# Projection evicted one image at a time, rows dealt by h mod 4, 1 KB runs and tables written in stage A, in a two-layer conv block

## The chip, the cores and the metric

The kernel runs on one core of one Trainium2 chip. The metric is the device time of one execution in microseconds. Before the change it is 4737.04 us, the median of three runs (4735.08 to 4738.93). Everything is float32.

A core has TensorE (PE, with its weight loads shown apart as PEld), VectorE (DVE), ScalarE (ACT), GpSimd (POOL) and SyncE (SP). In this kernel SP and POOL do little but issue DMAs. DMAs issued on SP and on POOL go through two queues that share the core's 16 DMA engines.

## The reference

The input `x` is (16, 192, 64, 64): 16 images, 192 channels, 64 rows `h`, 64 columns `w`.

```python
# layer 0
h = layernorm_over_channels(x, eps=1e-6) * ln1_w + ln1_b
projected, gate = split(conv1x1(h, in_proj_w) + in_proj_b)       # 192 -> 384
projected = depthwise3x3(projected, dw_k)                        # zero padded
decay  = clip(sigmoid(decay_logits), 0.05, 0.995)                # 4 x 192
mix    = softmax(mix_logits, axis=0);  iscale = 1 + tanh(input_scale)
# s[i] = decay*s[i-1] + (1-decay)*iscale*projected[i]
scanned = mix[0]*scan_right + mix[1]*scan_left + mix[2]*scan_down + mix[3]*scan_up
mixed = (scanned + depthwise3x3(projected, le_k)) * sigmoid(gate)
mixed = gelu(batchnorm_over_images_and_pixels(mixed, eps=1e-5) * bn_w + bn_b)
x = x + conv1x1(mixed, out_proj_w) + out_proj_b
h2 = layernorm_over_channels(x)
x = x + fc2(gelu(fc1(h2)))                                       # 192 -> 768 -> 192
# layer 1
t = relu(bn(mean_over_pixels(x) @ w1.T));  taps = t @ w2.T + b2  # per image
x = depthwise3x3(x, taps * mask) + bias                          # 4 of 9 taps are not 0
```

The batch norm needs all images before any pixel can go on, so the kernel has one full stop between the part in front of it and the part behind it.

## The kernel before

**Set-up (L107 to L195).** The 192 channels lie as three classes of 64. Biases, decays and gains are worked out from the parameter table; `wi` (the projection's weights, scaled by the layer norm's weights, with the mean taken off) is made; `bias_bc` (L144) holds the projection's bias on all partitions. Depthwise taps, local taps and the two horizontal scans are written as eight vectors of 128 per channel (`gv`, `gt`), from which banded 64x64 matrices can be read by an overlapping access pattern; they are stored to DRAM as `dv_d` (3 stores, L192) and `lv_d` (5 stores, L194) on the SP queue.

**Stage A (L197 to L265).** The work is cut into 64 chunks: two images, one in each half of the partitions, by 8 rows (512 pixels). `load_a` (L208) brings a chunk on SP with two DMAs of 2 KB runs into one of three `xa` buffers, issued two chunks ahead. `stat_a` (L218) transposes it on TensorE and takes the layer norm's statistics on VectorE. `project` (L235) does four groups of 128 pixels: one PSUM tile `ps_pj` of two banks holds both images, the output has pixels on the partitions and 384 channels along a row. Of each image VectorE evicts the projected half with scale and bias (`stt`, L246, which the profile shows at L64), ScalarE the gate half (L247), so both engines read the same bank. Results go to `stg`, two tiles of [128, 384, 16] per block; a block is four chunks (32 rows of two images). When a block is complete, four DMAs on POOL (L252) store it to `pg_d` with 24 KB per partition. A partition holds a column `w` and the parity of the row: row 32 jb + 2 j + parity.

**Stage B (L268 to L398).** 24 groups of 8 channels, 96 iterations of two channels each; now `w` is on the partitions, eight images in each half. `load_b` (L285) loads a group on SP: four DMAs of `pg_d` with 512 byte runs into `p_b` and `g_b`, and the tables `dm` (L299) and `lm` (L302); two buffers of each. One iteration has: `depthwise` (L305), seven parts of banded matmuls (L324 to L328, run by L315) into two `ps_d` tiles, copied to `q` by ScalarE (L331); `scans` (L334), the two vertical scans on VectorE (L343, L345) with a decay table written by ScalarE (L339); `local` and `vertical` (L354, L362, run by L352), which add the local taps, both horizontal scans and both vertical scans in `ps_l`; `gate` (L366), the sigmoid (L373), the product into `o_b` (L377) and the batch norm's statistics (L378). After four iterations two DMAs on POOL (L382) store the group to `mixed_d`.

**Batch norm and stage C (L401 on).** The statistics are put together (L408 to L437), then the pool `early` is closed (L438), and in the space that this frees the weights of the rest are loaded on SP (L440 to L459), with a few products made from them (L470 to L478). Stage C goes over 64 chunks of two images by 8 rows: load of x and of mixed (y), out projection, layer norm, fc1, gelu, fc2, and per image the second layer's taps.

**What sets the order.** TensorE's instructions run in the order in which the code issues them (`manual_schedule(engines=PE_ORDER)`); a tile scheduler orders VectorE and ScalarE by readiness. DMAs of one queue are issued in order, and an issue that has to wait for a free buffer holds back what is behind it on SP or POOL.

Of the kernel before, what the change touches and what calls it, by code (L numbers as in the profile page):

```python
# [21 lines left out]
F32 = mybir.dt.float32  # L22
# [21 lines left out]
AR = CR // 2  # L44

# [7 lines left out]
def conv_block_kernel(ctx: ExitStack, tc: tile.TileContext, x, prm, w_in, w_out, w_fc1, b_fc1, w_fc2, w1, bn1, w2, out):  # L53
# [22 lines left out]
    pg_d = dram.tile([n_img_all, NB, HW, 2 * C * BR], F32, tag="pg_d", name="pg_d")  # L76
# [7 lines left out]
    load_cls3(pt3, prm)  # L84

# [6 lines left out]
    eps5 = cp.tile([128, 1], F32, tag="eps5", name="eps5")  # L92
    nc.vector.memset(eps5, 1e-5)
# [3 lines left out]
    bias_bc = ce.tile([128, 2 * C], F32, tag="bias_bc", name="bias_bc")  # L97
    dec_b = ce.tile([128, 2, C // 2], F32, tag="dec_b", name="dec_b")
    stats = ce.tile([128, C, 6], F32, tag="stats", name="stats")


    with ExitStack() as stage:
        ka = stage.enter_context(tc.tile_pool(name="ka", bufs=1))
        wi = ka.tile([128, 3, 2 * C], F32, tag="wi", name="wi")
        load_cls3(wi, w_in)

        with tc.tile_pool(name="ps_set", bufs=1, space=PSUM) as ps0, tc.tile_pool(name="sset", bufs=1) as sp:  # L107
            lo = slice(0, 64)

# [21 lines left out]
            dg = sp.tile([64, 3, 4, 64], F32, tag="dg", name="dg")  # L131
            lnb = sp.tile([64, 3, 128], F32, tag="lnb", name="lnb")
            for t in range(3):
                for k, v in enumerate((pt3[lo, t, INB:INB + 1], pt3[lo, t, GTB:GTB + 1], dec[:, t, 2:3], dec[:, t, 3:4])):
                    nc.vector.tensor_scalar_mul(dg[:, t, k], ident[lo, lo], v)
                nc.vector.tensor_scalar_mul(lnb[:, t], ones[lo], pt3[lo, t, LN1B:LN1B + 1])
            pb = ps0.tile([128, 2 * C], F32, tag="pb", name="pb")
            for t in range(3):
                nc.tensor.matmul(pb, lnb[:, t], wi[lo, t], start=(t == 0), stop=False)
            for t in range(3):  # L140
                for k in range(2):
                    c0 = k * C + 64 * t
                    nc.tensor.matmul(pb[:, c0:c0 + 64], ones[lo], dg[:, t, k], start=False, stop=(t == 2 and k == 1))
            nc.vector.tensor_copy(bias_bc, pb)  # L144
            pd = ps0.tile([128, 2, C], F32, tag="pd", name="pd")
            for t in range(3):
                for k in range(2):
                    nc.tensor.matmul(pd[:, k, 64 * t:64 * t + 64], ones[lo], dg[:, t, 2 + k],
                                     start=(t == 0 and k == 0), stop=(t == 2 and k == 1))

            for i, q in enumerate(HALF):
                nc.vector.tensor_copy(dec_b[q].rearrange("p k (g c) -> p k g c", c=GC // 2),
                                      pd[q].rearrange("p k (g i c) -> p k g i c", i=2, c=GC // 2)[:, :, :, i])


            for t in range(3):
                nc.vector.tensor_scalar_mul(wi[:, t], wi[:, t], pt3[:, t, LN1W:LN1W + 1])
# [3 lines left out]
            for t in range(3):  # L161
                nc.tensor.matmul(pc, mean_w, wi[lo, t], start=(t == 0), stop=(t == 2))
            for t in range(3):
                nc.vector.tensor_sub(wi[:, t], wi[:, t], pc)
# [20 lines left out]
            gt = sp.tile([128, 8, C], F32, tag="gt", name="gt")  # L185
# [5 lines left out]
            for k in range(3):  # L191
                nc.sync.dma_start(dv_d[:, k].rearrange("g s c -> s g c"), gt[:, k].rearrange("s (g c) -> s g c", c=GC))  # L192
            for k in range(5):
                nc.sync.dma_start(lv_d[:, :, k].rearrange("g i s c -> s (g i) c"),  # L194
                                  gt[:, 3 + k].rearrange("s (g c) -> s g c", c=GC // 2))  # L195
# [8 lines left out]
        xr = x.rearrange("b (t p) h w -> b p t (h w)", p=64)  # L204
# [3 lines left out]
        def load_a(n):  # L208
            p, c = divmod(n, NCH)
            xa = xp.tile([128, 3, CH], F32, tag="xa", name="xa")  # L210
            for i, q in enumerate(HALF):
                nc.sync.dma_start(xa[q], xr[2 * p + i, :, :, c * CH:(c + 1) * CH])
# [22 lines left out]
        def project(n):  # L235
# [3 lines left out]
            for g in range(AR):  # L239
                ps = psa.tile([128, 2, CH], F32, tag="pj", name="ps_pj", bufs=2)  # L240
                for t in range(3):
                    for i, q in enumerate(HALF):
                        nc.tensor.matmul(ps[:, i, 0:2 * C], pixels(n, t, g)[q], wi[q, t], start=(t == 0), stop=(t == 2))  # L243
                for i in range(2):
                    j, r = part * AR + g, ast[n]["rs"][:, g, i:i + 1]
                    stt(stag[blk][i][:, 0:C, j], ps[:, i, 0:C], r, bias_bc[:, 0:C])  # L246
                    nc.scalar.activation(stag[blk][i][:, C:2 * C, j], ps[:, i, C:2 * C], AF.Identity, scale=r)  # L247
            if part == per - 1:
                p, jb = divmod(blk, NB // 2)
                for i in range(2):  # L250
                    for par, q in enumerate(HALF):
                        nc.gpsimd.dma_start(pg_d[2 * p + i, 2 * jb + par], stag[blk][i][q].rearrange("p o j -> p (o j)"))  # L252
                stag.pop(blk)

        with tc.manual_schedule(engines=PE_ORDER):
            for n in range(-1, n_ac):
# [7 lines left out]
                if n >= 0:  # L264
                    project(n)  # L265


    with ExitStack() as stage:  # L268
        kb = stage.enter_context(tc.tile_pool(name="kb", bufs=1))

        mask = kb.tile([128, 2, 2 * CH], F32, tag="mask", name="mask")
        nc.vector.memset(mask, 1.0)
        for k, r in ((0, 0), (1, HW - 1)):
            nc.vector.memset(mask[:, k].rearrange("p (i h) -> p i h", h=HW)[:, :, r:r + 1], 0.0)
# [6 lines left out]
        n_blk = n_half * NB  # L281
# [3 lines left out]
        def load_b(g):  # L285
            s = grp[g]
            s["p"] = gp.tile([128, n_blk, GC, BR], F32, tag="pb", name="p_b")
            s["g"] = gp.tile([128, n_blk, GC, BR], F32, tag="gb", name="g_b")
            for k, dst in ((0, s["p"]), (1, s["g"])):
                lo = (k * C + g * GC) * BR  # L290
                for i, q in enumerate(HALF):
# [431 lines left out]
```

## Time and profile before

| what | value |
|---|---|
| median of the runs | 4737.04 us |
| the profiled execution: its time; its span | 4739.38 us; 4737.6 us |
| set-up, to the first statistics matmul | 0 to 82 us |
| stage A, compute | 82 to 1031 us |
| nothing but DMA | 1031 to 1083 us |
| stage B, 96 iterations | 1083 to 1890 us |
| batch norm, weights, first chunk | 1890 to 1987 us |
| stage C | 1987 to 4738 us |
| busy, share of the span: PE, PEld, DVE, ACT, POOL | 84, 38, 55, 37, 4% |
| mean granted TensorE clock | 0.942 |
| DMA | 500.35 MB, 106 GB/s over the span |

In the profile, a group is named by its line, engine, operation and tiles as output<-inputs, with the mean length of one instruction and what ended the idle time before it. A releaser "DMA xa<-in_x_dram" means that the engine waited for that load. The granted clock is the share of full speed that TensorE was given. The DMA share is the mean busy share of the 16 DMA engines; it can come out slightly above 1.

### The profile page before, as it was taken

Reading aid. Unit: us, or ns where it says so; the run is one execution under the profiler, and the core shown is the slowest. Engines: PE = TensorE matmul, PEld = TensorE weight load, DVE = VectorE, ACT = ScalarE, POOL = GpSimd, SP = SyncE. Lnnn points to the kernel's source line nnn. Section 1 sums busy time; section 2 is a strip of 40 time slices with the busy share of each in tenths; the row PEclk is TensorE's granted clock in tenths of the full one; section 3 lists DMA queues with packets and bytes.
Section 4 is the critical chain, followed back from the end, with each engine's and each line's share of the span. In section 5 each row is a group of like instructions: output and inputs, shape, how many; then the busy total and the mean of one; then the engine's idle time right before and its main releaser. Section 6 shows DMA issues by size and latency. Waiting matters only on the chain.

```text
span 4737.6 us, 59020 instructions
## 1 busy us (share of the span) xinstructions
PE 3959.5 (84%) x24876; PEld 1779.4 (38%) x24876; DVE 2619.0 (55%) x3862; ACT 1753.0 (37%) x2045; POOL 201.6 (4%) x336
## 2 busy tenths in 40 slices
PE   4666766648999998499989999899899899999990
PEld 2444434425555555133333333333333333333330
DVE  3444444436888888344554644744745645546427
ACT  1333333324555555133333433333433333334322
POOL 0000000000000000000000000100100000000001
PEclk9888898888999999699999999999999999999995
DMA  9555666559999996311221221311311212212103
GB/s 46 160 160 160 160 160 160 160 138 230 228 236 237 231 241 152 96 34 47 60 70 37 71 58 38 93 35 47 87 39 48 74 47 58 72 38 66 48 1 98
DMA packets 381896, 500.35 MB, mean 106 GB/s; under 512 B 55056, under 2 KB 268304, under 8 KB 377536
## 3 DMA queue, kind: packets, MB, share of 16 engines
q1 hardware_dynamic: 346496, 289.99, 27.9%
q0 software_dynamic: 35136, 206.59, 15.9%
q8 instruction: 196, 3.21, 0.3%
q14 instruction: 68, 0.56, 0.0%
HBM read 289.17 MB, written 207.36 MB: 105 GB/s over the span
## 4 chain that ended last, share of the span: by engine, by line
PE 45%; DVE 19%; ACT 5%; DMA 5%; issue 3%; SPq 1%; POOL 0%; ACTq 0%; DVEq 0%; POOLq 0%
PE ps_f L584 19%; PE ps_f L506 17%; PE ps_o L506 6%; DVE o L64 5%; DVE v L345 4%; DVE v L343 4%; DMA out_dram<-o 3%; DVE o_b L377 2%; ACT q L331 2%; ACT sg L373 2%; PE ps_m L506 1%; DVE stats L378 1%; ACT o L644 1%; PE ps_v L506 1%; DMA y<-mixed_d 1%
## 5 line engine op out<-in xcount | busy, mean ns | idle before, releaser
L584 PE MATMUL ps_f<-h,wf 64*128 64x512 f32 x4608 | 1054.4, 604 | 17.1 <-DVE h L574 17.1
L506 PE MATMUL ps_f<-gl,wf 128*64 128x512 f32 x4608 | 1021.5, 592 | 0.0
L584 PEld LDWEIGHTS ps_f<-h,wf 64*128 64x128 f32 x4608 | 437.2, 189 | 638.4 <-issue 579.4
L243 PE MATMUL ps_pj<-wi,xa 64*128 64x384 f32 x3072 | 545.9, 502 | 105.1 <-ACT stg L247 105.1
L506 PEld LDWEIGHTS ps_f<-gl,wf 128*64 128x64 f32 x4608 | 330.5, 137 | 658.9 <-issue 658.1
L587 ACT ACTIVATE gl<-ps_f,bf 128x1024 f32<-128x1024 f32 x384 | 425.1, 1109 | 320.7 <-PE ps_f L584 319.9
L545 DVE SCALAR_TENSOR_TENSOR ximg<-ps_o,pt,x 128x512 f32<-128x512 f32 x192 | 144.1, 751 | 610.8 <-PE ps_o L506 610.8
L64 DVE SCALAR_TENSOR_TENSOR o<-ximg,taps,o 128x1024 f32<-128x1024 f32 x318 | 402.2, 1278 | 95.6 <-ACT o L644 91.0
L243 PEld LDWEIGHTS ps_pj<-wi,xa 64*128 64x128 f32 x3072 | 294.2, 192 | 331.4 <-ACT stg L247 154.8
L64 DVE SCALAR_TENSOR_TENSOR stg<-ps_pj,rsa,bias_bc 128x192 f32<-128x192 f32 x512 | 265.2, 535 | 273.0 <-ACT stg L247 166.2
L506 PE MATMUL ps_o<-mx,wo 128*64 128x512 f32 x1536 | 380.9, 617 | 40.8 <-ACT mx L536 14.0
L247 ACT ACTIVATE stg<-ps_pj,rsa 128x192 f32<-128x192 f32 x512 | 287.3, 583 | 301.4 <-DVE stg L64 297.4
L573 DVE RECIPROCAL rs<-rs 128x512 f32<-128x512 f32 x64 | 214.5, 3352 | 297.6 <-ACT rs L572 297.6
L315 PE MATMUL ps_d<-p_b,dm 64*64 64x256 f32 (+3 forms) x5376 | 300.6, 366 | 57.4 <-DMA dm<-dv_d 57.4
L339 ACT ACTIVATE tab<-mask,dec_b 128x1024 f32<-128x1024 f32 x192 | 220.4, 1149 | 319.0 <-DVE v L343 221.8
L315 PEld LDWEIGHTS ps_d<-p_b,dm 64*64 64x64 f32 x5376 | 267.7, 196 | 142.2 <-issue 140.8
L343 DVE TENSOR_TENSOR_SCAN v<-tab,q 128x1024 f32<-128x1024 f32 x96 | 220.1, 2292 | 175.9 <-ACT q L331 175.9
L223 PE MATMUL ps_xt<-ident,xa 128*128 128x128 f32 x768 | 119.4, 316 | 236.6 <-DMA xa<-in_x_dram 233.8
L228 DVE BATCH_NORM_STATS2 st<-ps_xt 128x6 f32<-128x192 f32 x512 | 165.8, 337 | 257.5 <-PE ps_xt L223 197.0
L352 PE MATMUL ps_l<-q,lm 64*64 64x504 f32 (+1 forms) x2304 | 275.9, 604 | 2.8 <-ACT q L331 2.8
L561 ACT ACTIVATE sq<-h 128x1536 f32<-128x1536 f32 x64 | 94.8, 1482 | 466.9 <-DVE h L558 466.9
L352 PE MATMUL ps_l<-v,lm 64*64 64x512 f32 x1536 | 211.9, 617 | 66.3 <-DVE v L345 66.2
(132 smaller groups left out, 2976.7 us busy)
## 6 DMA issues: line engine op xcount, KB each, us to landing
pg_d<-stg POOLq DMA_DIRECT2D x64, 1536.0 KB, 19.8
out_dram<-o POOLq DMA_DIRECT2D x212, 256.0 KB, 3.7
xa<-in_x_dram SPq DMA_DIRECT2D x128, 384.0 KB
p_b<-pg_d SPq DMA_DIRECT2D x48, 1024.0 KB
g_b<-pg_d SPq DMA_DIRECT2D x48, 1024.0 KB
mixed_d<-o_b POOLq DMA_DIRECT2D x48, 1024.0 KB, 12.4
x<-in_x_dram SPq DMA_DIRECT2D x128, 384.0 KB
y<-mixed_d SPq DMA_DIRECT2D x128, 256.0 KB
```

The source lines that it names most:

```text
L64: nc.vector.scalar_tensor_tensor(o, in0, scalar, in1, ALU.mult, ALU.add, **kw)
L243: nc.tensor.matmul(ps[:, i, 0:2 * C], pixels(n, t, g)[q], wi[q, t], start=(t == 0), stop=(t == 2))
L247: nc.scalar.activation(stag[blk][i][:, C:2 * C, j], ps[:, i, C:2 * C], AF.Identity, scale=r)
L315: nc.tensor.matmul(dst(ps[ih][o]), s["dm"][q, di + 1, :, ch], src(s["p"][q, :, ch]), start=(di == 0), stop=stop)
L339: nc.scalar.activation(tab, mask[:, d], AF.Copy, scale=dec_b[:, d, k:k + 1])
L343: nc.vector.tensor_tensor_scan(vf, tab, q, 0.0, ALU.mult, ALU.add)
L345: nc.vector.tensor_tensor_scan(vf[:, ::-1], tab[:, ::-1], q[:, ::-1], 0.0, ALU.mult, ALU.add)
L352: nc.tensor.matmul(dst(bst[k]["ps"][i][o]), grp[g]["lm"][q, m, :, c], src(q, ih), start=start, stop=stop)
L506: nc.tensor.matmul(ps[q], w(i), rhs(i), start=start, stop=stop)
L573: nc.vector.reciprocal(rs, rs)
L584: nc.tensor.matmul(pf[:, i], wf1[q, t, 128 * m:128 * m + 128], s["h"][q, t], start=(t == 0), stop=(t == 2))
L587: nc.scalar.activation(gl, pf, AF.Gelu, bias=bf1[:, m:m + 1])
```

## The change

It touches set-up, stage A, stage B and the place where the weights of stage C are loaded. Line numbers behind "now" are those of the changed kernel.

- **Rows.** Rows are dealt by h mod 4 in place of parity: block `u` of a pair of images holds rows 4 j + 2 u + r, r on the partition halves. A chunk's 512 pixels are now four pairs of neighbouring rows, so its x load has 512 byte runs and is split into six DMAs.
- **Eviction.** Each image has its own PSUM tile and is evicted whole, 384 channels in one instruction: image 0 by VectorE (now L357), image 1 by ScalarE (now L358), with the scale only.
- **Bias.** The projection's bias moves behind the depthwise conv: constant values pass through the conv as the sum of its taps, and differ in the first and last row and column. Set-up works out `bias_q` (inside, correction for the first row, for the last row), and ScalarE's copy of `ps_d` to `q`, one instruction now, adds it, with two small instructions for the edge rows (now L449, L451). `bias_g` keeps the gate's bias.
- **Layout.** The channels' order in `pg_d` is group by group, projected beside gate, so that stage B's runs are 1 KB. `pg_d` is split in two tensors: groups 0 and 1, and the other 22; a block is stored by eight DMAs in place of four. Group 0 is fetched back during stage A into its own buffer, `pg_even`, by `fetch_pair` (now L160) on POOL, one DMA per pair of images.
- **Stage B's buffers and order.** Three buffers hold projected and gate together; the product is written over the projected part, and the store leaves from there, so there is no `o_b`. Loads run two groups ahead. The depthwise conv has five parts in place of seven. It runs two iterations ahead of `vertical` and `gate` where it ran one ahead, and the scans of an iteration come before the next depthwise.
- **Set-up and weights.** The eight stores to `dv_d` and `lv_d` and the weights of stage C are issued inside stage A's loop; products made from the weights (`finish_weights`) too. Space for the weights is no longer shared with stages A and B.

The diff, cut to its core:

```diff
+    def load_weights():            # the loads that stood behind early.close()
+        ...
+    def finish_weights(pb):        # s1, the sums pb, bf1 and wf1: unchanged statements
+        ...
+    pg_even = pf.tile([128, n_blk, 2, GC, BR], F32, tag="pg_e", name="pg_e")
+    def fetch_pair(p):
+        q, i0 = HALF[2 * p // n_half], 2 * p % n_half
+        nc.gpsimd.dma_start(pg_even[q, i0 * NB:(i0 + 2) * NB].rearrange("p n k c j -> p n (k c j)"),
+                            pg_d[0][2 * p:2 * p + 2, :, :, 0:GE].rearrange("i b w e -> w (i b) e"))
...
+            for k in range(3):
+                pr = ps0.tile([3, C], F32, tag="pb", name="pr")
...
+                pq = ps0.tile([128, C], F32, tag="pd", name="pq")
+                nc.tensor.matmul(pq, indt, svt, start=True, stop=True)
+                by_half(bias_q[:, k], pq)
...
-            for k in range(3):
+        def store_vectors(k):
+            if k < 3:
                 nc.sync.dma_start(dv_d[:, k].rearrange("g s c -> s g c"), gt[:, k].rearrange("s (g c) -> s g c", c=GC))
...
-        xr = x.rearrange("b (t p) h w -> b p t (h w)", p=64)
+        xr = x.rearrange("b (t p) (j u r) w -> b u p t j (r w)", p=64, u=2, r=2)
...
             for i, q in enumerate(HALF):
-                nc.sync.dma_start(xa[q], xr[2 * p + i, :, :, c * CH:(c + 1) * CH])
+                for t in range(3):
+                    nc.sync.dma_start(xa[q, t].rearrange("p (g n) -> p g n", n=128),
+                                      xr[2 * p + i, u, :, t, part * AR:(part + 1) * AR])
...
-                for i in range(2):
-                    j, r = part * AR + g, ast[n]["rs"][:, g, i:i + 1]
-                    stt(stag[blk][i][:, 0:C, j], ps[:, i, 0:C], r, bias_bc[:, 0:C])
-                    nc.scalar.activation(stag[blk][i][:, C:2 * C, j], ps[:, i, C:2 * C], AF.Identity, scale=r)
+                j, rs = part * AR + g, ast[n]["rs"]
+                nc.vector.tensor_scalar_mul(stag[blk][0][:, :, j], ps[0], rs[:, g, 0:1])
+                nc.scalar.activation(stag[blk][1][:, :, j], ps[1], AF.Copy, scale=rs[:, g, 1:2])
             if part == per - 1:
...
+                for d, o0, o1 in ((0, 0, GF * 2 * GC), (1, GF * 2 * GC, 2 * C)):
+                    for i in range(2):
+                        for par, q in enumerate(HALF):
+                            nc.gpsimd.dma_start(pg_d[d][2 * p + i, 2 * u + par],
+                                                stag[blk][i][q, o0:o1].rearrange("p o j -> p (o j)"))
+                if u == 1 and p >= 1:
+                    fetch_pair(p - 1)
+                if p == n_pairs - 1 and u == 1:
+                    fetch_pair(p)
...
                     project(n)
+                if n == 3:
+                    load_weights()
+                if 8 <= n < 16:
+                    store_vectors(n - 8)
+                if n == 16:
+                    finish_weights(psa.tile([128, NFC], F32, tag="pb2", name="pb2"))
...
+            s["pg"] = pg_even if g % 3 == 0 else pg_odd[g % 3 - 1]
...
+            blocks = lambda a: a.rearrange("p (i b) j -> p i b j", b=NB)
+            rows4 = lambda a: a.rearrange("p (i j b) -> p i b j", b=NB, j=BR)
+            part(0, blocks, rows4)
+            part(-1, lambda a: blocks(a)[:, :, 0:NB - 1], lambda a: rows4(a)[:, :, 1:NB])
+            part(-1, lambda a: blocks(a)[:, :, NB - 1, 0:BR - 1], lambda a: rows4(a)[:, :, 0, 1:BR])
...
-            for ih in range(2):
-                nc.scalar.copy(q[:, ih], ps[ih])
+            edge = lambda a, r: a.rearrange("p k (i h) -> p k i h", h=HW)[:, :, :, r]
+            nc.scalar.activation(q, ps, AF.Identity, bias=bias_q[:, 0, k:k + 1])
+            for e, r in ((1, 0), (2, HW - 1)):
+                nc.scalar.activation(edge(q, r), edge(ps, r), AF.Identity, bias=bias_q[:, e, k:k + 1])
...
-            load_b(0)
-            for k in range(-1, n_bp + 1):
+            for g in range(3):
+                load_b(g)
+            for k in range(-2, n_bp + 1):
                 if k >= 1:
                     vertical(k - 1)
                     gate(k - 1)
-                if k + 1 < n_bp:
-                    if (k + 1) % hp_ == 0 and (k + 1) // hp_ + 1 < NCG:
-                        load_b((k + 1) // hp_ + 1)
-                    depthwise(k + 1)
+                    if k % hp_ == 0 and k // hp_ + 2 < NCG:
+                        load_b(k // hp_ + 2)
+                if 0 <= k + 1 < n_bp:
                     scans(k + 1)
+                if k + 2 < n_bp:
+                    depthwise(k + 2)
                 if 0 <= k < n_bp:
                     local(k)
```

The scheduler moves issues that wait for nothing: in the changed program as built, SP's first DMAs are the parameters and `w0`, the weights, three `dv_d` and two `lv_d` stores, then the x loads of chunks 0 to 2, then the other three `lv_d` stores.

## The prediction

> **What bounds the kernel now.** I read the mean of each engine by stage first (busy time in given stretches), because one share over the whole span hides three stages with different limits. Columns: stretch and its length, busy us (instructions) of PE, PEld, DVE, ACT, POOL; then granted clock, DMA share, GB/s. Stage A is 82 to 1031 us, B 1083 to 1890, C 1987 to the end.
>
> ```profile
> ...
> 40.00:80.00 40.00, 0.00 (x0) 0.00 (x0) 0.00 (x0) 0.00 (x0) 0.00 (x0) 1.00 1.48 21
> ...
> 300.00:500.00 200.00, 142.21 (x836) 85.86 (x838) 96.03 (x347) 66.12 (x125) 8.49 (x16) 0.90 0.56 150
> ...
> 1031.00:1083.00 52.00, 0.02 (x2) 0.05 (x2) 0.00 (x0) 5.38 (x6) 0.76 (x2) 0.51 1.01 209
> ...
> 1300.00:1500.00 200.00, 182.56 (x2320) 110.64 (x2312) 169.90 (x146) 116.45 (x145) 13.03 (x12) 1.00 1.03 235
> ...
> 2400.00:4600.00 2200.00, 2097.47 (x9672) 756.23 (x9674) 1153.36 (x1254) 783.90 (x705) 77.54 (x146) 0.98 0.19 54
> ```
>
> Stage C is TensorE at 95%; no line of its loop changes. A is 71% TensorE with nothing else full: it waits. B has TensorE at 91% and VectorE at 85%, coupled. 40 to 80 us and 1031 to 1083 us have no compute at all.
>
> Next, order of time on TensorE in A (start, length, line, count, idle before and what ended it):
>
> ```profile
> 375.27 1.53 PE L223 MATMUL ps_xt<-ident,xa 128*128 128x128 f32 x12
> 376.73 4.14 PE L243 MATMUL ps_pj<-wi,xa 64*128 64x384 f32 x24
> 382.73 5.83 PE L243 MATMUL ps_pj<-wi,xa 64*128 64x384 f32 x24 [1.86 <-ACT stg L247]
> 388.49 1.53 PE L223 MATMUL ps_xt<-ident,xa 128*128 128x128 f32 x12
> 389.95 4.14 PE L243 MATMUL ps_pj<-wi,xa 64*128 64x384 f32 x24
> 395.90 4.14 PE L243 MATMUL ps_pj<-wi,xa 64*128 64x384 f32 x24 [1.81 <-ACT stg L247]
> 411.17 2.79 PE L223 MATMUL ps_xt<-ident,xa 128*128 128x128 f32 x12 [11.13 <-DMA xa<-in_x_dram]
> ```
>
> Two waits are seen. In each chunk TensorE waits about 1.8 us for an eviction: the whole list of waits has ScalarE waiting for VectorE's half of the same bank 436 times (297.4 us). And once per block of four chunks the x load is late: 178.6 us in 15 times. The DMA queues say why. In 388 to 394 us only the 24 KB store packets move (1.40 MB). In the next ten us:
>
> ```profile
> q0 software_dynamic: 116, 2.36, 93.0%
> q1 hardware_dynamic: 148, 0.29, 7.6%
> ```
>
> (packets, MB, share): the load gets about one 2 KB packet for each 24 KB store packet, so it lands when the store burst is over, 35.9 us after the block's boundary at 375.27. The load issued at 375.3 is through by 381, since the stores only flow from 379.9.
>
> In B I read one iteration (8.29 us):
>
> ```profile
> 1407.72 2.27 DVE L345 TENSOR_TENSOR_SCAN v<-tab,q 128x1024 f32<-128x1024 f32 x1
> ...
> 1408.28 1.04 PE L352 MATMUL ps_l<-v,lm 64*64 64x512 f32 x8
> ...
> 1410.05 1.15 PE L352 MATMUL ps_l<-v,lm 64*64 64x512 f32 x8 [0.73 <-DVE v L345]
> ...
> 1411.02 3.08 PE L315 MATMUL ps_d<-p_b,dm 64*64 64x512 f32 x56
> ...
> 1413.81 2.29 DVE L343 TENSOR_TENSOR_SCAN v<-tab,q 128x1024 f32<-128x1024 f32 x1 [1.19 <-ACT q L331]
> ...
> 1413.93 2.82 PE L352 MATMUL ps_l<-q,lm 64*64 64x512 f32 x24
> ```
>
> VectorE waits 1.19 us for q, q for the depthwise matmuls, these for the second vertical product, and that (0.73 us) for the scan: a ring through three engines, though none is full.
>
> **The change, part by part**, against this execution: 4739.38 us, of which the span is 4737.6 and 1.8 lies around it; the median shown (4737.04) is 2.3 lower.
>
> *Setup and start of A.* Before, the 8 table stores with 16 and 32 byte packets keep the DMA busy from 20 to 72 us and the first x load lands at 82.4. Moved into A, they are not all gone from the front: in the changed program's SP order the 11 weight loads (beside the 3 of pv, there before), then 3 dv_d and 2 lv_d stores still stand ahead of the first x load. Rate: 44 us for 5 lv_d = 8.8 each, 8 us for 3 dv_d. The set-up arithmetic grows (about 45 small DVE rows at 0.13 us, and three rounds TensorE to VectorE at about 2 us, worked side by side with the rest): from 27.6 to an estimated 36 us. The weights, 2.2 MB at some 235 GB/s = 10 us, fit in the idle DMA time at 8 to 20 us. First x: 38 + 2 x 8.8 + 4 = 60, so -22. The other 3 lv_d (26 us) stand between x chunks 2 and 3; chunk 3 lands at about 99 and is wanted at 85: +14. With a chunk that is 1.3 us shorter four times (below), the first block boundary comes at 121 in place of 135.3: -14. Ends: -30 (set-up no longer) and +5 (all 8 stores ahead of x).
>
> *Eviction.* Per chunk 8 stt (535 ns) and 8 activations (583) of 192 become 4 tensor_scalar and 4 activations of 384, one image each, from their own banks. VectorE, 384 from PSUM into 64 byte steps: between 557 (contiguous copy, L144) and 1082 (twice the strided 192); I take 750, as the strided 192 is nearer to a contiguous 192 (355) than ScalarE's is. ScalarE: 475 (between its contiguous 192 at 319 and 512 at 578) to 1166; I take 1000, since its strided 192 costs 264 more than its contiguous one. Neither engine fills the chunk: VectorE 4 x 0.75 + 2.8 statistics, ScalarE 4.3. TensorE: 1.46 + 4 x 2.03 = 9.6 us; its third group needs the first bank at 5.5, which ScalarE frees at 4.9 + 1.0: 0.5 lost. Chunk 11.5 -> 10.2.
>
> *The x loads and the block.* But the block's length is set by the late load: 35.9 + two chunks = 59.7 on average ((1030.4 - 135.3)/15). Bytes of the burst stay 6.3 MB. SP issues 6 DMAs per chunk in place of 2 (3.7 us in place of 1.2; SP waits most of the time for buffers) and 1536 packets of 512 B; POOL issues 8 stores per block in place of 4 (4.3 us; POOL is idle 95%) and 8 fetches in all, 0.5 MB each, behind the stores: +1 us per block. 512 B packets move at 215 GB/s (stage B, 1412 to 1418 us: 218), 2 KB ones at 229 (82 to 88): no loss worth counting outside the burst. So the first load of the burst (needed after 10.2 us) still slips in ahead of the 22 KB stores (from about 6.1 us), the second lands at 36, and the block is 36 + 2 x 10.2 + 0.5 = 57: 15 x -2.7 = -40. If the first is caught too, the block is 30 + 3 x 10.2 = 60.6: +14. If the burst shortens, 54.5: -78.
>
> The Trainium skill, DMA: Bandwidth & Descriptors, Queues, rings and completion order, says that an engine round-robins between queues by packet. The rows above show nearly that (148 against 116); by it a load with quarter-size packets gets a quarter of the bytes in a burst, which speaks for the caught case and a total of about 4631.
>
> *A to B.* Before 52.6 us: store landing (27.2), 4 MB of group 0, tables. After: landing 27, then the tables (2 x 0.7 MB, first pair about 5 us) beside the last fetch, as group 0's other seven eighths are already in SBUF: 33. Group 1 (4.2 MB at 230 = 18 us, tables 4) comes about 3 us late. -16; ends -26 and 0.
>
> *B.* Parts of the depthwise go from 7 to 5: 16 of 56 matmul instructions with 8 columns go, the 1520 columns stay. By rows, 512 columns take 0.88 us, so 2.6 of the 2.91 is columns: 0 to 0.3 saved, 0.15 taken. The scan moves one iteration away: in the built order VectorE runs scan k+2 next to gate k, so the ring is cut; TensorE's own sum is 2.64 + 1.04 + 0.97 + 2.91 = 7.56, less 0.15 = 7.4; VectorE's is 7.05. ScalarE: q once 1.13 (row 1109 to 1149 for 1024) for 2 x 0.576, plus two of 16 elements at 0.2 to 0.3, 2 x 1.15, 2 x 0.83 = 5.6: covered. DMA per group of four: 4.2 MB pg at 215 to 230, 2.1 MB stores and 1.4 MB tables partly beside each other at 385: 29 to 31 us against 29.6 wanted. It is just covered; if not, 7.75 per iteration. I take 7.45: 96 x -0.84 = -81 (ends 7.2: -105; 7.75: -52). New wait: a load must await the landing (12.4 us) of the store from the same buffer; it is due 44 us after that store's issue, and 12.4 + 19.5 + 4 = 36.
>
> *B to C.* 11 weight DMAs (SP, 1902.2 to 1908.8) and their TensorE sums go; y follows x at once: issued about 9 us earlier, -9 (0 to -15). The moved finish, some 4 us on TensorE at chunk 16, falls into a chunk that has the load's wait behind it: 0, or +4 without that cover.
>
> Sum: -14 - 40 - 16 - 81 - 9 = -160: 4737.6 - 160 + 1.8 - 2.3 = **4577 us**.
>
> The Trainium skill, PSUM — Partial Sum Buffer, Specifications (TRN2), has 8 byte lines and any non-contiguous matmul output much slower. In the iteration above L315 with step 2 takes 589 ns for 512 columns, as contiguous L352 does, so the row wins; by the page a step of 4 that doubled the 2.6 us would give 10 us per iteration and about 4820.
>
> **Rivals.** (1) The first load of each burst is caught by the stores, -40 becomes +14: 4631. For: one-for-one packets. Against: its 0.77 MB needs 3.6 us and flows some 4 us before the large stores. 0.22. (2) DMA becomes B's bound at 31 us a group: 4606. For: share 1.03 now. Against: dips to 0.2 in each group (1420 to 1422 us). 0.13. (3) Slower: in-place buffers put store, load and tables in series: 12.4 + 19.5 + 6.7 (4.2 and 1.4 MB at 215) + 4 of latencies = 42.6 us a group in place of 33.2, +226, for 4737 + 226 - 79 = 4884. It decides from 36.5 us a group (33.2 + 79/24). Against: three buffers leave the load 44 us. 0.05. (4) The order of B's engines is not what cuts the ring and B stays at 8.29: 4658. 0.04.
>
> **How the numbers follow.** Forecast 0.56 (4500 to 4610, the free ends of setup, block and pace), rivals 0.22, 0.13, 0.05, 0.04. The range 4505 to 4645 leaves out the slower case, (4), and the far ends of the forecast. Within 0.2% (some 9.5 us, about what this measurement tells from no change) I put 0.02, since no one case ends there; slower 0.06, faster 0.92.
>
> **What would show it.** Right: in A no wait of ScalarE for VectorE's stg, chunks of 10.2, one x wait per block; in B 7.4 to 7.5 per iteration and no wait of VectorE for q; first projection near 60 us; gap before B near 33. Wrong: two x waits per block or one right after the burst's first chunk (1); waits of L436 for pg (2, 3); longer L436 matmuls (PSUM step).

## The result: slower by 2.8%, and where the 131 us went

The changed kernel takes 4871.36 us (median of 4 runs, 4867.46 to 4873.69) against 4737.99 for the kernel before (4 runs): a ratio of 1.0279, 95% interval 1.0261 to 1.0296. The forecast was 4577 with a range of 4505 to 4645, so sign and size were wrong. The profiled execution of the changed kernel has a span of 4868.6 us, 131.0 more than before. By stages, with the boundaries read from the first store of a block, the first depthwise product, the last group's store of stage B and the first fc1 product (the prediction had taken other marks around stage A of the kernel before, 135.3 and 1030.4 us, so its lengths differ by up to 4 us):

| stretch | before | after | change | forecast |
|---|---|---|---|---|
| start to the first block's stores | 136.9 | 118.6 | -18.3 | -14 |
| fifteen blocks of stage A | 891.4 | 953.1 | +61.7 | -40 |
| last block's stores to the first depthwise product | 54.7 | 38.1 | -16.6 | -16 |
| stage B | 806.3 | 922.8 | +116.5 | -81 |
| to the first fc1 product | 97.6 | 88.9 | -8.7 | -9 |
| stage C | 2750.7 | 2747.1 | -3.6 | 0 |

Three of the five terms came close to what was worked out. Two have the wrong sign: the block of stage A and the iteration of stage B.

The busy time by stage, the same view as before with the changed kernel's stretches (31 to 57 us is the wait for the first x load, 1072 to 1109 the gap ahead of stage B):

```profile
31.00:57.00 26.00, 0.90 (x6) 0.55 (x6) 0.00 (x0) 0.96 (x3) 0.00 (x0) 1.00 1.44 47
300.00:500.00 200.00, 138.65 (x813) 88.21 (x811) 83.53 (x276) 51.12 (x65) 13.90 (x27) 0.81 0.58 151
1072.00:1109.00 37.00, 0.00 (x0) 0.00 (x0) 0.23 (x3) 3.01 (x3) 4.51 (x9) 0.53 0.83 199
1300.00:1500.00 200.00, 168.25 (x1672) 105.48 (x1672) 143.24 (x126) 124.95 (x147) 10.86 (x10) 1.00 1.03 204
2400.00:4600.00 2200.00, 2089.86 (x9678) 754.29 (x9676) 1202.89 (x1300) 798.72 (x718) 87.17 (x168) 0.98 0.22 58
```

In stage B TensorE fell from 182.6 to 168.3 us in 200, VectorE from 169.9 to 143.2, and the transfers from 235 to 204 GB/s at the same busy share, 1.03. All three went down together, so none of them reads as the new bound. In stage A the granted clock is 0.81 where it was 0.90.

TensorE's order of time over one block boundary of stage A (columns as before):

```profile
434.53 1.53 PE L334 MATMUL ps_xt<-ident,xa 128*128 128x128 f32 x12
435.99 8.34 PE L354 MATMUL ps_pj<-wi,xa 64*128 64x384 f32 x48
444.26 0.66 PE L334 MATMUL ps_xt<-ident,xa 128*128 128x128 f32 x4
459.69 1.12 PE L334 MATMUL ps_xt<-ident,xa 128*128 128x128 f32 x4 [14.78 <-DMA xa<-in_x_dram]
468.87 1.09 PE L334 MATMUL ps_xt<-ident,xa 128*128 128x128 f32 x4 [8.06 <-DMA xa<-in_x_dram]
469.89 9.71 PE L354 MATMUL ps_pj<-wi,xa 64*128 64x384 f32 x48
```

The stores of the block are issued at 435.5. A chunk of projection now runs through without a wait for an eviction. But the very next chunk's load is caught: its first third is there at 444, the rest comes at 459.7 and 468.9, 33.4 us behind the boundary (30 to 35 us in all fifteen blocks). The block is 33.4 + 3 x 9.7 + 0.6 = 63.1 us; 63.5 is the average. The wait also lowers the clock: the granted share is 0.50 from 449.5 to 473.3 us, and the projection of the chunk behind the wait takes 9.71 us in place of 8.32. The DMA queues from 446 to 456 us show how the load is held (packets, MB, share):

```profile
q0 software_dynamic: 144, 2.52, 99.5%
q1 hardware_dynamic: 143, 0.07, 2.4%
```

One load packet per store packet, as before, but a load packet is now 512 bytes: 0.07 MB in 10 us.

One iteration of stage B in the order of time, VectorE, ScalarE and TensorE (lines between left out):

```profile
1416.44 2.27 DVE L466 TENSOR_TENSOR_SCAN v<-tab,q 128x1024 f32<-128x1024 f32 x1
...
1418.75 1.15 ACT L459 ACTIVATE tab<-mask,dec_b 128x1024 f32<-128x1024 f32 x1 [1.20 <-DVE v L466]
...
1419.81 1.10 ACT L449 ACTIVATE q<-ps_d,bias_q 128x1024 f32<-128x1024 f32 x1
1420.93 0.45 ACT L451 ACTIVATE q<-ps_d,bias_q 128x16 f32<-128x16 f32 x2
1421.42 2.29 DVE L464 TENSOR_TENSOR_SCAN v<-tab,q 128x1024 f32<-128x1024 f32 x1 [2.70 <-ACT q L451]
1421.44 2.91 PE L436 MATMUL ps_d<-pg_o,dm 64*64 64x512 f32 x40 [1.51 <-ACT q L451]
```

The iteration is 9.56 us, every time the same: a ring. The depthwise product that q copies had ended at 1405.3, 14 us earlier (the one from 1411.88 is the next, and the one at 1421.44 in the last line waits until this q gives its PSUM tile back). Yet q starts at 1419.81: ScalarE works in order, and ahead of q in its queue stands a decay table that waits until the scan L466 gives its buffer back. That table (in the built order of ScalarE) belongs to the iteration behind q's. So VectorE's own chain (scan, two products, two statistics, scan) is followed by table, q and two edge instructions, 2.70 us in which VectorE does nothing. The sigmoids lie beside this ring, not on it.

With this in mind the profile of before reads differently. ScalarE there, in the iteration that the prediction shows:

```profile
1410.03 1.15 ACT L339 ACTIVATE tab<-mask,dec_b 128x1024 f32<-128x1024 f32 x1 [1.03 <-DVE v L345]
1411.08 1.74 ACT L373 ACTIVATE sg<-g_b,bias_bc 128x512 f32<-128x512 f32 x2
1412.72 1.05 ACT L331 COPY q<-ps_d 128x512 f32<-128x512 f32 x2
```

q has no wait in brackets: it waited for nothing but its place in the queue, behind a table that waited for the scan. The prediction had led the ring through TensorE's products.

### The profile page after: what moved, and what is told of

Same layout as the page of the kernel before. It is cut to its first block, busy times and chain, and to the rows that moved or that the text cites. A ratio compares the mean times of both kernels' runs of the same rounds, so it can differ in the third digit from the quotient of the medians.

```text
span 4868.6 us, 55793 instructions
## 1 busy us (share of the span) xinstructions
PE 4010.1 (82%) x23368; PEld 1840.1 (38%) x23368; DVE 2565.6 (53%) x3657; ACT 1810.9 (37%) x1885; POOL 237.4 (5%) x412
## 4 chain that ended last, share of the span: by engine, by line
PE 43%; DVE 7%; DMA 4%; issue 2%; ACT 1%; SPq 0%; POOL 0%; ACTq 0%; POOLq 0%; DVEq 0%
PE ps_f L665 18%; PE ps_f L587 17%; PE ps_o L587 6%; DVE o L65 5%; DMA out_dram<-o 3%; PE ps_m L587 1%; ACT o L725 1%; PE ps_v L587 1%; DMA y<-mixed_d 1%; DVE mx L616 1%; SPq L609 0%; DVE ximg L626 0%; POOL out_dram L729 0%; DMA mixed_d<-pg_o 0%; PE ps_k L587 0%
## 5 line engine op out<-in xcount | busy, mean ns | idle before, releaser
L354 PEld LDWEIGHTS ps_pj<-wi,xa 64*128 64x128 f32 x3072 | 320.8, 196 | 208.5 <-issue 37.4
L473 PE MATMUL ps_l<-q,lm 64*64 64x504 f32 (+1 forms) x2304 | 331.6, 608 | 4.8 <-DVE pg_o L499 4.5
L357 DVE TENSOR_SCALAR stg<-ps_pj,rsa 128x384 f32<-128x384 f32 x256 | 226.0, 883 | 188.6 <-PE ps_pj L354 188.1
L358 ACT ACTIVATE stg<-ps_pj,rsa 128x384 f32<-128x384 f32 x256 | 237.2, 928 | 200.9 <-PE ps_pj L354 197.6
L436 PE MATMUL ps_d<-pg_o,dm 64*64 64x384 f32 (+2 forms) x2560 | 194.2, 436 | 95.5 <-ACT q L451 89.0
L334 PEld LDWEIGHTS ps_xt<-ident,xa 128*128 128x128 f32 x768 | 94.1, 156 | 409.8 <-DMA xa<-in_x_dram 306.4
L729 POOL DMA_DIRECT2D out_dram<-o x212 | 110.0, 523 | 2692.3 <-DVE o L65 2689.1
## 6 DMA issues: line engine op xcount, KB each, us to landing
pg_d<-stg POOLq DMA_DIRECT2D x64, 1408.0 KB, 18.3
```

What stands on the lines that cost most here:

```text
L334: nc.tensor.transpose(xt[:, t, g], pixels(n, t, g), ident)
L354: nc.tensor.matmul(ps[i], pixels(n, t, g)[q], wi[q, t].rearrange("p g k c -> p (g k c)"), start=(t == 0), stop=(t == 2))
L357: nc.vector.tensor_scalar_mul(stag[blk][0][:, :, j], ps[0], rs[:, g, 0:1])
L358: nc.scalar.activation(stag[blk][1][:, :, j], ps[1], AF.Copy, scale=rs[:, g, 1:2])
L473: nc.tensor.matmul(dst(bst[k]["ps"][i][o]), grp[g]["lm"][q, m, :, c], src(q, ih), start=start, stop=stop)
```

## Experiments

Theories. For stage A: *load form* (512 byte packets are caught by the burst) against *stores* (eight stores and the fetches hold any load). For stage B: *order* (the ring through ScalarE's queue) against *DMA* (share 1.03), *buffers*, and the loop's order. Kernels are the changed one with one edit, unless said; each has one run, e12 four, and runs of the kernel before beside them took 4724.63 to 4743.65 us.

**ScalarE's order (e1).**

```diff
-        with tc.manual_schedule(engines=PE_ORDER):
+        with tc.manual_schedule(engines=PE_ORDER | {mybir.EngineType.Activation}):
             for g in range(3):
```

> The changed kernel, with ScalarE's instructions of stage B also kept in the order of the source, so that q stands behind its own iteration's tables and not behind the next but one's. Theory order (an iteration of 9.56 us is a ring: scan L466, the table that waits for its buffer, q queued behind that table, the two edge instructions, scan L464): q is no longer behind a table that waits, the iteration falls to 7.4 to 7.8 us (TensorE's own sum is 7.4, VectorE's 7.05), 96 x about 2.05 less, 4675 us. Rival DMA (stage B is bound by its transfers, whose share is 1.03 at 203 GB/s): the iteration stays above 9.3 us and the time above 4845 us. Between the two (8 to 9 us, 4720 to 4820) both would bind, one behind the other.

Measured: 4762.33 us, 109 less, a little over half of what the theory gave. Single iterations went down to 6.89 us, and the scan no longer waits for q; but about every second group TensorE waits for a load. From the order of time of this run, one such wait and two scans of an undisturbed stretch:

```profile
1404.45 5.62 PE L436 MATMUL ps_d<-pg_e,dm 64*64 64x512 f32 x34 [10.38 <-DMA dm<-dv_d]
...
1422.43 2.29 DVE L464 TENSOR_TENSOR_SCAN v<-tab,q 128x1024 f32<-128x1024 f32 x1
...
1429.31 2.29 DVE L464 TENSOR_TENSOR_SCAN v<-tab,q 128x1024 f32<-128x1024 f32 x1
```

Groups take 27.6 and some 40 us in turn, 34.0 on average (first to last but one store of the stage, over 22), where the changed kernel has 38.2 and the kernel before 33.2. The ring was the bound, and a second limit lies 4 us below it.

**A third table buffer (e2).** `tab` with `bufs=3`.

> The changed kernel with three buffers of each decay table in place of two. Rival buffers (the table waits only because two buffers are too few): the wait goes, 7.5 us per iteration, 4675 us. Theory order: in the built order the scheduler uses the third buffer to put the tables one more iteration ahead, the table in front of q again waits for the scan just run, and the iteration stays at 9.5 to 9.6 us, 4870 us.

Measured: 4866.14 us, the same pace as the changed kernel. The table in front of q waits for the scan as before:

```profile
1408.14 1.15 ACT L459 ACTIVATE tab<-mask,dec_b 128x1024 f32<-128x1024 f32 x1 [1.21 <-DVE v L466]
```

So a third buffer does not take the wait away: the scheduler puts the tables ahead as far as buffers go, and a table still waits in front of q.

**The loop's old order (e3).**

```diff
-                if 0 <= k + 1 < n_bp:
-                    scans(k + 1)
-                if k + 2 < n_bp:
-                    depthwise(k + 2)
+                if k + 1 < n_bp:
+                    depthwise(k + 1)
+                    scans(k + 1)
```

> The changed kernel with stage B's loop in the order of before: depthwise conv one iteration ahead, its scans behind it. Theory order: the iteration goes back to that of before, 8.3 us, or up to 8.7 since q with its edges takes 1.5 us on ScalarE where two copies took 1.15: 4870 - 96 x (0.85 to 1.25) = 4750 to 4790 us. Rival DMA, or the buffers in which the product overwrites the projected part: the loop's order doesn't matter, 9.4 to 9.6 us, 4855 to 4875 us.

Measured: 4848.96 us, 9.33 us per iteration, outside both. VectorE still waits for q, 2.23 us. Here the ring is that of before with dearer pieces behind the scan: table, two sigmoids (2.25 us in place of 1.74), q and edges (1.55 plus the gaps in place of 1.05): 8.29 + 0.51 + 0.5. So of the 1.27 us that an iteration lost, by way of this kernel about 1.0 come from ScalarE's longer instructions on the ring, which the bias and the new layout brought, and 0.2 from the loop's order. Other ways of splitting it are possible, since the changed kernel's ring has other pieces: the sigmoids are off it, and the gate's products and statistics (1.26 and 1.27 us) have come between the scans.

**The kernel before with ScalarE's order mended (e8).** The same edit in the kernel before.

> The kernel before, with ScalarE's instructions of stage B kept in the order of the source (q ahead of its own iteration's tables). Theory order (the 8.29 us of before are a ring of the two scans, a table that waits for the second, two sigmoids and q behind it in ScalarE's queue): the iteration falls to the next limit, TensorE's 7.56 or the DMAs' 31 to 33 us a group, 7.7 to 8.2 us, 4735 - 96 x (0.1 to 0.6) = 4675 to 4725 us. Theory of the prediction (the ring goes from the scan through TensorE's vertical and depthwise products to q) and rival DMA (235 GB/s is all that there is): 8.25 to 8.3 us, 4728 to 4740 us.

Measured: 4668.23 us beside 4743.65 for the kernel before on the same chip, 1.6% faster, groups of 30.4 us, 7.6 an iteration. ScalarE's q now waits for the depthwise product, and stands ahead of the tables:

```profile
1402.58 1.07 ACT L331 COPY q<-ps_d 128x512 f32<-128x512 f32 x2 [3.76 <-PE ps_d L315]
...
1404.73 2.29 DVE L343 TENSOR_TENSOR_SCAN v<-tab,q 128x1024 f32<-128x1024 f32 x1 [1.28 <-ACT tab L339]
```

This is one line, and worth 70 to 75 us (stage B itself is 70 shorter), where the whole change was forecast to gain 81 in stage B. It also shows that before, at a DMA share of 1.03 and 235 GB/s, the transfers were not the bound: here they reach 255 GB/s in the same stretch, 1300 to 1500 us.

**Two x loads, and six, of 2 KB runs (e4, e5).** Eight neighbouring rows per chunk as before, so that rows stand in the wrong places while the amount of work is the same; e5 keeps six DMAs. The edit of e4:

```diff
-        xr = x.rearrange("b (t p) (j u r) w -> b u p t j (r w)", p=64, u=2, r=2)
+        xr = x.rearrange("b (t p) h w -> b p t (h w)", p=64)
...
-                for t in range(3):
-                    nc.sync.dma_start(xa[q, t].rearrange("p (g n) -> p g n", n=128),
-                                      xr[2 * p + i, u, :, t, part * AR:(part + 1) * AR])
+                nc.sync.dma_start(xa[q], xr[2 * p + i, :, :, c * CH:(c + 1) * CH])
```

> The changed kernel with stage A's x loads as before: two DMAs of 2 KB runs per chunk, that is 8 neighbouring rows; the rows then stand in the wrong places and the output is not the reference's. Theory load form (six DMAs of 512 byte packets are still moving when the store burst begins, and are caught by it): the first load of a burst slips through again and the second is caught one chunk later; block 63.5 -> about 36 + 2 x 9.7 + 0.6 = 56 us, 15 x -7.5 = -112, about 4758 us. Rival stores (the eight stores or the fetches hold the loads, whatever their form): blocks stay at 63 to 64 us, 4860 to 4875 us.

> The changed kernel with stage A's x loads of 8 neighbouring rows (2 KB runs, rows in the wrong places, the output is not the reference's), but still six DMAs per chunk. The run with two such DMAs gave 4758.7 us, the changed kernel 4871. Theory packets (a 512 byte packet gets one turn against one store packet): six DMAs of 2 KB packets do as well as two, blocks of 56 us, 4755 to 4765 us. Theory issues (six issues at 0.62 us bring the last piece 2.5 us later, into the burst): blocks stay near 63 us, 4855 to 4875 us. Between: both count.

Measured: 4758.73 and 4742.02 us, blocks of 56.5 and 55.2 us on average (first to last of the sixteen stores, over 15). The forecast's 57 is there as soon as the packets are 2 KB, and six issues cost nothing in sum. In e4 the first load behind the boundary at 341.6 us slips through, and the next one is caught:

```profile
350.32 1.53 PE L333 MATMUL ps_xt<-ident,xa 128*128 128x128 f32 x12
351.78 8.32 PE L353 MATMUL ps_pj<-wi,xa 64*128 64x384 f32 x48
375.71 2.79 PE L333 MATMUL ps_xt<-ident,xa 128*128 128x128 f32 x12 [15.61 <-DMA xa<-in_x_dram]
```

In e5 the last pieces of the first load are still caught in every block, but they are through 15 to 24 us behind the boundary in place of 30 to 35 (here 18.5, behind 341.7):

```profile
360.25 1.09 PE L334 MATMUL ps_xt<-ident,xa 128*128 128x128 f32 x4 [6.00 <-DMA xa<-in_x_dram]
```

So six DMAs let the load be caught; the size of the packet sets what that costs, not the eight stores or the fetches, which are the same in all three kernels.

**Five x buffers (e6).** The right rows, 512 byte runs.

```diff
-        xp = stage.enter_context(tc.tile_pool(name="xa", bufs=3))
+        xp = stage.enter_context(tc.tile_pool(name="xa", bufs=5))
...
-                if 0 <= n and n + 2 < n_ac:
-                    load_a(n + 2)
+                if 0 <= n and n + 4 < n_ac:
+                    load_a(n + 4)
```

> The changed kernel with five x buffers in place of three, loads issued four chunks ahead in place of two. Theory caught load (the load issued as the burst begins lands 33.4 us behind the block's boundary and is wanted after one chunk): it is wanted after three chunks, so the block falls to 33.4 + 9.7 + 0.6 = 43.7 us, if the DMA engines carry the block's 9.4 MB in that time (215 GB/s): 15 x -19.8 = -297, 4575 us. Rival lanes (SP has eight DMAs outstanding at most, and a chunk takes six, so the loads behind a caught one aren't issued): the caught chunk still comes 33 us behind the boundary and the next one right behind it, at least one more chunk is gained but not two: 48 to 55 us, 4640 to 4745 us.

Measured: 4566.54 us, blocks of 44.1 us on average. The caught load still takes as long, but three chunks of work stand in front of it. TensorE at a boundary of this run:

```profile
401.61 8.31 PE L354 MATMUL ps_pj<-wi,xa 64*128 64x384 f32 x48
409.85 0.66 PE L334 MATMUL ps_xt<-ident,xa 128*128 128x128 f32 x4
413.07 0.63 PE L334 MATMUL ps_xt<-ident,xa 128*128 128x128 f32 x4 [2.56 <-DMA xa<-in_x_dram]
413.94 0.63 PE L334 MATMUL ps_xt<-ident,xa 128*128 128x128 f32 x4 [0.25 <-DMA xa<-in_x_dram]
414.50 8.33 PE L354 MATMUL ps_pj<-wi,xa 64*128 64x384 f32 x48
```

The limit of eight outstanding DMAs can be seen in SP's queue, which waits 17 times between 105 and 770 us for an earlier x load to land (30.4 us in all, the longest 4.1), but it costs the block little: the theory without it gave 43.7 us.

**The eviction of before on top of five buffers (e11).**

```diff
-                nc.vector.tensor_scalar_mul(stag[blk][0][:, :, j], ps[0], rs[:, g, 0:1])
-                nc.scalar.activation(stag[blk][1][:, :, j], ps[1], AF.Copy, scale=rs[:, g, 1:2])
+                for i in range(2):
+                    nc.vector.tensor_scalar_mul(stag[blk][i][:, 0:C, j], ps[:, i, 0:C], rs[:, g, i:i + 1])
+                    nc.scalar.activation(stag[blk][i][:, C:2 * C, j], ps[:, i, C:2 * C], AF.Copy, scale=rs[:, g, i:i + 1])
```

> The kernel with five x buffers (4566.5 us, blocks of 41 us) with the eviction of before: each image's projected half by VectorE and its gate half by ScalarE out of one tile of two banks, the scale only. Theory eviction (shared banks cost 1.8 us of each chunk, which the late load hid in the changed kernel and nothing hides here): chunk 9.7 -> 11.5, block 41 -> 46.5, 16 x 5.5 = +88, 4655 us; up to 4682 if all 64 x 1.8 count. Rival (TensorE waited for ScalarE because of the bias on VectorE, 535 ns, or the transfers set the block): less than +25, below 4592 us.

Measured: 4608.85 us, 42 more than e6 (beside them the kernel before took 4727.27 and 4743.65), between the two: the chunk is 11.5 us again, and ScalarE waits for VectorE in the list of waits from 200 to 800 us:

```profile
ACT stg L359 <- DVE stg L358: 244.8, 352, 3.9
```

The block is 46.9 us in place of 44.1, read from the traces: 15 x 2.8 = 42. So one image per engine, each from its own bank, saves 1.8 us per chunk, bias or not, and of 7.1 us per block 2.8 come through even with five buffers, because the loads take most of the rest.

**Stage B's second limit (e7, e9, e10, e13, e14).** All with ScalarE's order mended (e1). e7 splits each load into projected and gate, 512 byte runs; e10 pads the rows of the larger tensor to 24 KB as before; e13 has the buffers of before (two of projected, gate and product each); e14 is e13 with e10's rows. e9 was a first form of e13 in which a gate's load is issued ahead of the last two sigmoids that need the buffer's old content: these read the wrong group and wait for it, so its 5128.11 us answer nothing.

> The first experiment's kernel (ScalarE in the order of the source) with each stage B load split into projected and gate, 512 byte runs in place of 1 KB; the gate's half then doesn't wait for the store of the product. Theory 1 KB (packets of 1 KB move at 190 to 203 GB/s in the traces of the changed kernel and the first experiment, those of 512 bytes before at 199 to 222): the 4.2 MB of a group take 19.5 us in place of 21.5, a group 31.7 in place of 33.7, 24 x -2 = -48, 4715 us. Rival row order or store wait (the slower rate isn't the packet's size): 4750 to 4770 us, as the first experiment's 4762.

> The first experiment's kernel (ScalarE in the order of the source, 4762 us, groups of 27.6 and 40.8 us in turn) with the buffers of before in the changed layout: two of projected, two of gate, two of the product, loads of 512 byte runs one group ahead. Theory buffers (a load that must wait for the landing of the product's store, 12 to 14 us, sets stage B once ScalarE's order is mended): groups even out at 30 to 31 us, as in the run of before with that order (29 to 31), 24 x -3.5 = -84, 4680 us. Rival layout (rows dealt by h mod 4 in two tensors are read more slowly, 190 to 200 GB/s, whatever the buffers): a group stays at 33 to 35 us, 4750 to 4790 us.

> The first experiment's kernel (4762 us) with the larger tensor padded from 22 to 24 groups, so that its rows stand 24 KB apart as before and not 22 KB; nothing else. Theory row distance (the distance makes reads of 1 KB go at 190 to 200 GB/s where before's went at 199 to 222): loads of a group 19.5 in place of 21.5 us, 24 x -2 = -48, 4715 us. Rival (the distance is nothing): 4755 to 4770 us, and the rate of loads alone stays below 203 GB/s.

> As the run with the buffers of before, but the gate's load of a group is issued only behind the last sigmoid of the group whose buffer it takes, and the projected part and tables two iterations earlier; the output is complete again. Theory buffers (a load that must wait 12 to 14 us for the landing of the product's store is what is left over 27.6 us): 30 to 31 us a group, 4680 us. Rival layout (loads of the changed layout at 190 to 200 GB/s set 33 to 35 us whatever the buffers): 4745 to 4790 us.

> The run with the buffers of before (4796.6 us) with the rows also 24 KB apart: ScalarE's order, buffers, 512 byte runs and row distance are now those of the kernel before with the mended order (7.55 us an iteration); what is left of the layout is the order of channels in a row, the second tensor and the rows dealt by h mod 4. Theory both (run length and row distance together make the slower loads; either alone changed nothing much): loads alone at 205 to 220 GB/s again, a group 30 to 31 us, 4680 us. Rival rest of the layout: loads alone stay at 182 to 203 GB/s, a group 34 to 36 us, 4770 to 4800 us.

Measured, with the rate of loads alone as the median over stretches of 2 us within stage B in which at most two store packets moved and the mean packet was under 1.2 KB:

| kernel | us | group, us | loads alone, GB/s |
|---|---|---|---|
| before | 4737.99 | 33.2 | 209 |
| e8, before, order mended | 4668.23 | 30.4 | 222 |
| after | 4871.36 | 38.2 | 193 |
| e1, order mended | 4762.33 | 34.0 | 190 |
| e7, 512 byte runs | 4803.36 | 34.9 | 186 |
| e10, 24 KB rows | 4754.80 | 33.3 | 190 |
| e13, buffers of before | 4796.60 | 35.4 | 188 |
| e14, both | 4791.59 | 35.3 | 187 |

Neither the run's length, nor the distance of the rows, nor the product written in place is the cause: each was put back, in e14 all three together, and the loads stayed at 186 to 190 GB/s. What sets the second limit is the transfers: from 1300 to 1500 us their share is 1.08 in e1, 1.09 in e13 and 1.10 in e14, at 225, 217 and 218 GB/s, where e8 has 255 at 1.11. Waits of a load for a store's landing are not the cause: e1's SP queue has 42 of them in stage B, 263 us in all, and e13's has none, yet e13 is no faster. TensorE there still waits for loads, in its list of waits (the longest is the gap ahead of stage B)

```profile
PE ps_d L442 <- DMA dm<-dv_d: 169.9, 19, 38.8
```

Why loads out of the new layout are slower (193 against 209 GB/s for the two kernels as they stand, 186 to 190 against 222 with ScalarE mended) stays open. Left of the difference are, among others, the order of channels in a row, the second tensor and the place of the tensors in DRAM; none of these was tried alone. The rows' deal changes which image rows a row of `pg_d` holds, but not where in it the loads read.

**All together (e12).** Five x buffers, ScalarE's order, 24 KB rows.

> The changed kernel with the three edits together: five x buffers in stage A, ScalarE of stage B in the order of the source, rows of the larger tensor 24 KB apart. If the two causes are independent (the caught load in stage A, the order of ScalarE's queue in stage B), the gains add: 4871 - 305 (five buffers) - 109 (order) - 8 (rows) = 4449 us, 4430 to 4470, a ratio to before of 0.939. If they aren't (a faster stage A leaves more for the gap before stage B, or stage B's second limit moves), 4480 to 4560 us.

Measured: 4452.79 us (4448.65 to 4457.31, 4 runs), ratio to before 0.9406, interval 0.9389 to 0.9424. The gains add up (4449 expected). By stages against before, from the profiled span of 4449.9: to the first block 101.5 (-35.4), fifteen blocks 652.8 (-238.6), gap 38.8 (-15.9), stage B 819.5 (+13.2), to fc1 89.5 (-8.1), stage C 2747.8 (-2.9). Stage B is still slower than before: what this kernel gains, it gains in stage A and on both sides of it.

## Why the prediction was wrong, step by step

- **Set-up and start of A: right.** First projection's statistics at 57.0 us (60 forecast), a stall of 12.0 at chunk 3 (14), first stores at 118.6 (121). The forecast -14 measured -18.3; its own terms, -22, +14 and four times -1.3, add up to -13.
- **Eviction: right in mechanism, sizes near.** VectorE 883 ns (750 taken), ScalarE 928 (1000 taken), chunk 9.72 (10.2 taken). (Twice the strided 535 ns is 1070, not the 1082 of the prediction's upper end; nothing hangs on it.) No wait of ScalarE for VectorE's half is left.
- **The block: wrong.** The step that failed is "So the first load of the burst ... still slips in ahead of the 22 KB stores". The load's rate outside a burst (215 GB/s) was right and beside the point. What counts is what it moves against one store packet: in its first 4 us (436 to 440) only 0.51 of its 0.77 MB went, since the small stores of `pg_d`'s first tensor were already moving, and then it moved 512 bytes a turn. This was rival (1), given 0.22, and its sign, a wait right behind the burst's first chunk, is there; its price was too low too, as the landing is 33.4 us behind the boundary and not 30. Here the rule of the Trainium skill, DMA: Bandwidth & Descriptors, Queues, rings and completion order, that was weighed against the row and set aside, had it right: turns go by packet, 143 against 144 in the rows above, so a quarter of the packet size is a quarter of the bytes.
- **A to B: right.** 38.1 us, -16.6 against -16.
- **B: wrong, and by most.** The step that failed is the reading of the ring ("VectorE waits 1.19 us for q, q for the depthwise matmuls"), and with it "The scan moves one iteration away ... so the ring is cut". In the changed kernel the depthwise product was ready 14 us before its q, and before, q waited for nothing either. The order of VectorE and TensorE was looked at, that of ScalarE was only summed ("5.6: covered"). A sum of busy time covers nothing on an engine that works in order, as these rows show ScalarE to do: q stands behind a table that waits. The sum was low too: a sigmoid out of the new layout takes 1.20 us and not 0.83, and by e3 ScalarE's longer instructions are worth 1.0 us where they lie on the ring. Rival (4), "the order of B's engines is not what cuts the ring", was near it, but had the old pace as its worst.
- **B's other terms.** Depthwise in five parts takes 2.90 us (2.76 taken). A step of four in PSUM did not slow it: 512 columns took 645 ns, where contiguous ones in the same stage (L473) took 603 to 645. The Trainium skill, PSUM — Partial Sum Buffer, Specifications (TRN2), says that any non-contiguous access slows matmuls significantly; the row, which was weighed against it, had it right here. TensorE's sum of 7.4 us was no floor: undisturbed iterations of e1 take 6.89, in which VectorE's instructions follow one another without a gap. "29 to 31 us against 29.6 wanted" for the DMAs was too low: groups come to 34 with ScalarE mended, with loads at 190 GB/s and not at 215 to 230. Without the ring, rival (2) would have held, at 8.5 us and not 7.75.
- **B to C, and C: right.** -8.7 against -9. Its products moved to chunk 16 leave no mark in the stage's sum.

## What to carry to other kernels

For every wait on a ring, look at what the instruction that ended it was doing before: no wait in brackets means that it stood in line, and then the engine's built order is to be read, not its busy time. An instruction that waits for a buffer far ahead can hold back one that is needed at once, and more buffers make it wait further ahead, not less; keeping the engine in the source's order cost one line and gave 1.6% in the kernel before and 2.2% in the changed one. Where a load and a store burst share the engines, count the load's packets, not its bytes, and put more chunks of work between its issue and its use.

## What was not expected of the hardware

- Longer runs did not make stage B's loads faster than before: 1 KB runs of the changed layout move at 190 to 193 GB/s, where 512 byte runs of the old layout moved at 209 to 222. The run's length is not what slows them, since 512 byte runs of the changed layout move at 186 to 188; the cause is not settled (above).
- Six DMAs of 2 KB packets did no worse than two (blocks of 55.2 and 56.5 us), although pieces of the first load are caught with six.
- A wait of some 23 us on TensorE takes its granted clock down: it averages 0.81 from 300 to 500 us where the kernel with five buffers has 0.97, and the projection of the first chunk behind the wait takes 9.71 us and not 8.32.
